# Seven products instead of eight for the queries of the first two units of an attention and low-rank layer

## The chip, the cores and the metric

The kernel runs on one core of a Trainium2 chip. The metric is the device time of one execution in microseconds (us); the median of three runs of the kernel before is 826.52 us (826.05 to 826.85). The engines of the core are TensorE (PE, with its weight loads as PEld), VectorE (DVE), ScalarE (ACT), GpSimd (POOL) and SyncE (SP), which here only issues transfers. Each engine works through its own instructions in the order in which they were written; engines wait for each other on semaphores.

## The reference

Two sequences of 512 tokens with 512 features pass a post-norm layer in float32:

```python
q = hidden_states @ Wq + bq          # 32 heads of 128
k = hidden_states @ Wk + bk          # 8 groups of 128, four heads share one
v = hidden_states @ Wv + bv
q = _rope(q, pos); k = _rope(k, pos)
ctx = softmax(causal(q @ k.T / sqrt(128))) @ v
x = layernorm(x + ctx @ Wo + bo)
y = x @ W_base.T + b_base            # plus low-rank terms of four active experts,
x = layernorm(x + y + contribs * alpha)  # weighted by a softmax of log(prior) + logits
```

## The kernel before, in words

**Units and slots.** A unit u is one group of heads in one of the two batches; there are 16, each with four heads of queries (R = 4). After a setup part, the order of all work is written out by hand: the function `slot(T)` issues, for each time slot T from -8 on, a few matrix products for PE and the small work of the other engines that belongs to them. The table `extra`, filled by `put(slot, f)`, adds work at the end of a slot. A unit's sixteen score blocks lie in slots 16u to 16u + 15; slots get longer as the causal width grows from 32 to 512 columns. Queries are projected about a unit ahead (`T + 24`), Wo's part of a unit begins at slot 16u + 21 (`wo_from`).

**Queries by eight or by seven products.** The queries of two heads are a 2 x 2 block product: weights (two heads by two halves of the features) times x (two halves of the features by two halves of the tokens). From unit 2 on this is done with seven block products instead of eight (`q_products`, steps numbered 1 to 7; each is two matrix products of 256 columns, in four instructions). They need sums of weight blocks (`w_sums`, four POOL instructions; the last overwrites a block of wq) and of x blocks (`x_sums`, four instructions per batch, tile xs). Step 1 begins the PSUM tile qx, step 2 the tile qy; steps 6, 7 and 4 add to qx; step 5 begins qy anew, step 3 adds to it. Between steps, qx is copied to SBUF by ACT (`q_copy`, names p1, u2, u3, c21) and qy is added to a copy by DVE (`q_sum`, names p1, u3, u2). A copy or sum must have read the PSUM tile before the next step overwrites or adds to it:

```python
product(halves[key]["qy"], w[:, 0], xs[:, b, 0], True)      # step 5
nc.vector.tensor_tensor(into, halves[u, k]["qy"], into, ALU.add)   # q_sum
```

The SBUF copies are tiles raw0 (two buffers) and raw1 (one). Units 0 and 1 instead use eight products: `q_mm`, four matrix products of 512 columns per head (two instructions each), in PSUM banks of `q_banks`.

**Rope.** `rope_step` has three parts on DVE (L368, L371, L375), one of which may work in place, and an add on POOL (L376) that writes qT or kT. Queries by eight products are read from PSUM (the program's name is pp), queries by seven from SBUF (name q).

**Setup.** SP issues the loads of x (first batch, four tiles), Wk, Wq of pair 0, the rope tables, Wq of pair 1, Wv, x of the second batch and more, in this order. POOL clears the tiles zt and then issues six small transfers: act_e, four of act_er, act_p, the indices of the active experts. PE transposes x of the first batch and projects K of unit 0; DVE does K's rope; `expert_rows` (eleven DVE instructions of integers, L232 to L252) makes row numbers out of act_e, act_er and act_p, and POOL gathers prior and router bias with them. Then the four heads of unit 0 are projected and roped, with V tiles 0 to 3 (`v_tile` on PE, `v_out` on ACT) and the transposes of the second batch in between. `gather_experts`, six gathers on POOL, is in slot -8.

**Other work around.** `prior_weights` has three steps: a logarithm on ACT, three small DVE instructions, and a small product on PE whose result DVE copies. They stand in slots -4, -3 and -2. `lora_weights` is in slots 12 and 16. V tiles 4 to 7 (second batch) stand in slots -1, 1, 3 and 5; Wv's next load, into the same buffer, in slot 6. `x_sums` of the first batch stand in slots 0 to 3, of the second in 12 to 15, on DVE. In slots 2 to 9 POOL adds bo to the eight tiles of x_sb (L885). `wo_sums` are four sums of Wo blocks per set of weights (L627). Sets 0 to 5 serve two units, the last four sets ("single") one unit each; `wo_sums` of sets 6 and 7 run on POOL one slot before the unit's Wo products, those of sets 0 to 5 on DVE.

Of the kernel before, what the change touches and what calls it, by code (L numbers as in the profile page):

```python
# [9 lines left out]
F32 = mybir.dt.float32  # L10
# [5 lines left out]
P = 128  # L16
# [13 lines left out]
def postln_layer_kernel(  # L30
# [248 lines left out]

    def lora_weights(step):  # L280
        if step == 0:
            ta = ps_wo.tile([P, KC, EAR + EA], F32, tag="wx", name="ta")
            for c in range(KC):
                nc.tensor.transpose(ta[:, c, :], ar_act[:, ts(c, P)], ident[: EAR + EA, : EAR + EA])
            nc.vector.tensor_copy(arT, ta)
            nc.vector.tensor_copy(b_jar, b_act.rearrange("p a (j r) -> p j a r", r=RK))
        else:

            tbm = ps_wo.tile([EAR, BJ, P], F32, tag="wx", name="tbm")
# [6 lines left out]
    def prior_weights(step):  # L296

        if step == 0:
            pr_eps = setup.tile([EA, 1], F32, name="pr_eps")
            nc.vector.tensor_scalar(pr_eps, pr_act, PRIOR_EPS, None, ALU.add)  # L300
            pr["lp"] = setup.tile([EA, 1], F32, name="lp")
            nc.scalar.activation(pr["lp"], pr_eps, AF.Ln)
        elif step == 1:
            lpb = setup.tile([EA, 1], F32, name="lpb")
            nc.vector.tensor_tensor(lpb, pr["lp"], rb_act, ALU.add)
            ones = setup.tile([EA, P], F32, name="ones")
            nc.vector.memset(ones, 1.0)
            pr["rep"] = setup.tile([EA, P], F32, name="lp_rep")
            nc.vector.tensor_scalar(pr["rep"], ones, lpb, None, ALU.mult)
        else:  # L310
            pl = ps_wo.tile([P, EA], F32, tag="wx", name="pl")
# [78 lines left out]
            k_of(u)  # L390
        rope_step(("k", u), H + unit(u)[0], part, kT[u])

    def q_mm(u, r, c, pool, tag):

        g, b = unit(u)
        proj_mm(("q", u, r), pool, tag, wqk["q", set_of(u), r // 2], ts(r % 2, D), b, c)

# [8 lines left out]
    ws = {}  # L406
    halves = {}

    def x_sums(b, step):
        b11, b12, b21, b22 = (  # L410
            xT[:, CH * k : CH * (k + 1), b * S + a * TH : b * S + (a + 1) * TH] for k in range(2) for a in range(2))
        t1, t2, t3, t4 = (xs[:, b, k] for k in range(4))
        nc.vector.tensor_tensor(
            *((t1, b12, b11), (t2, b22, t1), (t3, b22, b12), (t4, b21, t2))[step], ALU.subtract)

    def w_block(n, k, head, c_half):
# [450 lines left out]
        for c in range(KC):  # L867
            v_mm(gg, t, c, pool, tag)

    put(T_BEGIN, gather_experts)  # L870
    for n, gg, t in [(2 * t - 1, 0, TPB + t) for t in range(TPB)] + [(2 * t + 11, 1, t) for t in range(TPB)]:
        put(n, lambda gg=gg, t=t: v_tile(gg, t, ps_wo, "wx"))
        put(n + 1, lambda gg=gg, t=t: v_out(gg, t))
    for n in range(TPB):
        put(n, lambda n=n: x_sums(0, n))
        put(n + 12, lambda n=n: x_sums(1, n))
    for k in range(3):
        put(-4 + k, lambda k=k: prior_weights(k))
        if k < 2:
            put(12 + 4 * k, lambda k=k: lora_weights(k))  # L880
    put(1, lambda: load_q(1, 1))
    put(6, lambda: load_wv(1))
    put(17, lambda: load_wo(1))
    for t in range(NT):
        put(2 + t, lambda t=t: nc.gpsimd.tensor_tensor(x_sb[:, t, :], x_sb[:, t, :], bo_bc, ALU.add))  # L885

    def q_from(u, k):

# [38 lines left out]
    for n in range(NSETS - 2):  # L927
        single = len(set_units(n)) == 1
        for k in range(4):
            put(wo_from(set_units(n)[0]) + (-1 if single else (0, 1, 1, 3)[k]),  # L930
                lambda n=n, k=k, engine=nc.gpsimd if single else nc.vector: wo_sums(n, k, engine))


    weigh_at = {}
# [13 lines left out]
    def slot(T):  # L948

        uq, step = divmod(T + 24, UNIT)  # L950
        kq, step = divmod(step, 8)
        now = B <= uq < NU
        if now and step != 7 and step != 4:
            q_products(uq, kq, {0: 2, 1: 6, 2: 5, 3: 7, 5: 4, 6: 3}[step])
        un, kn = (uq, 1) if kq == 0 else (uq + 1, 0)
        if B <= un < NU and step == 7:
            q_products(un, kn, 1)
        plain_q = T - T_BEGIN < UNIT and divmod(T - T_BEGIN, QB)
        if plain_q:
            r, c = plain_q  # L960
            q_mm(1, r, c, *q_banks[r])
        uk, l = divmod(T + UNIT, UNIT)
        if 0 < uk < PLAIN_K and l < KC:
            k_mm(uk, l)
        kv, o = kv_at(T)
        if kv and o in KV_STEPS:
            kv_products(*kv, KV_STEPS[o])
        kw, sw = divmod(T - LAG_WO, 8)
        products = 0 <= kw < LAST // 8
        if products:  # L970
            wo_products(kw, sw)
# [12 lines left out]
        if kv and KV_OUT.get(o) in KV_ON_ACT:  # L984
            kv_out(*kv, KV_OUT[o])
        for part, j in weigh_at.get(T - 1, ()):
            if j == parts[part][1]:
                context_out(part)

        if 0 <= T - 3 < T_END:  # L990
            normalise(T - 3)
        if 0 <= T - 1 < T_END:
            masked_max(T - 1)
            exponentials(T - 1)
        if products:
            wo_adds(kw, sw)
        if sw == 0 and 0 < kw <= LAST // 8:
            wo_adds(kw - 1, 8)
        if now and step in (1, 5, 7):
            q_sum(uq, kq, {1: "p1", 5: "u3", 7: "u2"}[step])  # L1000
        if kv and o in KV_OUT and KV_OUT[o] not in KV_ON_ACT:
            kv_out(*kv, KV_OUT[o])
        if 0 <= T - 2 < T_END:
            reciprocals(T - 2)
        if 0 <= T - 4 < T_END:
            blocks_transposed(T - 4)
            if (T - 4) % QB == QB - 1:
                blocks_out((T - 4) // QB)
        if T % QB == 1 and 0 <= T // QB - 2 < NP:
            blocks_in(T // QB - 2)  # L1010
        if 0 <= (T - LAG_WO + 1) // 8 < LAST // 8 and (T - LAG_WO + 1) % 8 == 0:
            ctx_sums((T - LAG_WO + 1) // 8)

        ur, sr = divmod(T + 24 - 7, UNIT)
        kr, sr = divmod(sr, 8)
        if B <= ur < NU and sr < 6:
            q_rope(ur, 2 * kr + (sr < 3), sr % 3)
        r, part = divmod(T - T_BEGIN - QB, QB)
        if 0 <= r < R and part < 3:
# [12 lines left out]
    q_banks = ((ps_q, "qx"), (ps_q, "qy"), (ps_q, "qx"), (ps_wo, "wy"))  # L1032

    idle = ps_sc.tile([P, 2 * P], F32, tag="sc", name="idle")
    for _ in range(3):
# [5 lines left out]
    nc.vector.tensor_copy(bqkT, tb)  # L1041
    for c in range(KC):
        k_mm(0, c)
    for part in range(3):
        k_rope(0, part)
    expert_rows()

    for r in range(R):
        for c in range(KC):
            q_mm(0, r, c, *q_banks[r])  # L1050
        for part in range(3):
            q_rope(0, r, part)
        if r == 2:
            for t in range(TPB, NT):
                transpose_token_tile(xT[:, :, ts(t, P)], x_sb[:, t, :], *spare[t % 2 + 2], nc.scalar.copy)
        elif r:
            v_tile(0, r // 2, *spare[r // 2 * 2])
            v_out(0, r // 2)
    for t in range(2, TPB):
        v_tile(0, t, *spare[t % 2 * 2])  # L1060
        v_out(0, t)

    T_SETUP = 20
    for T in range(T_BEGIN, T_SETUP):
# [189 lines left out]
```

## Time and profile before

| what | value |
|---|---|
| median of the runs (lowest to highest) | 826.52 us (826.05 to 826.85) |
| the profiled execution's own time | 826.17 us |
| its span in the profile | 824.2 us |
| PE, DVE, ACT, POOL busy | 814.9, 598.2, 379.0, 327.8 us |
| 8.0 to 34.6 us (setup after the first transposes): PE, DVE, POOL busy | 26.3, 13.3, 10.6 of 26.6 us |
| 34.6 to 45.5 us (slots -8 to -1): PE, DVE, POOL busy | 10.9, 4.5, 8.8 of 10.9 us |
| 45.5 to 68.2 us (slots 0 to 11): PE, DVE, POOL busy | 22.7, 17.3, 15.8 of 22.7 us |
| 68.2 to 101.4 us: PE, DVE, POOL busy | 33.2, 27.0, 10.8 of 33.2 us |

A line of the profile's lists gives a source line, an engine, an operation, the tile written and the tiles read, and a duration. A line of the chain of work gives the start and the duration in us and what ran; the chain is followed back from the last instruction, at each step to what released it. A line of the waits names who waited for whom, the total in us, how often, and the longest. "[1.31 <-POOL wt L627]" at the end of a line is the idle time before it and what ended that. A line of the transfers ends in the time from issue to landing in us.

### The profile page before, as it was taken

What the parts mean: (1) busy time and instruction counts of PE and PEld (TensorE: products, weight loads), DVE (VectorE), ACT (ScalarE), POOL (GpSimd) and SP (SyncE); (2) the same over time, 40 slices, a digit from 0 to 9 for tenths busy, and PEclk for the clock granted to TensorE, in tenths of its full rate; (3) what the DMA queues carried; (4) which work ended last, traced back from release to release, by engine and by line L of the source; (5) the groups of instructions that cost most, each with busy time, mean ns of one, the idle gap of its engine ahead of it and who ended that gap; (6) DMA issues with size and microseconds to landing.
All of it is one profiled execution on the core that took longest, in us unless ns stands there. A gap on an engine that the chain in (4) does not pass through costs nothing.

```text
span 824.2 us, 11178 instructions
## 1 busy us (share of the span) xinstructions
PE 814.9 (99%) x3381; PEld 596.9 (72%) x3381; DVE 598.2 (73%) x1964; ACT 379.0 (46%) x1058; POOL 327.8 (40%) x374
## 2 busy tenths in 40 slices
PE   9999999999999999999999999999999999999997
PEld 5567777777777778777777878777777777655565
DVE  5368877687879886787867786787867678973445
ACT  1236453553545454545535454445535454563254
POOL 6464343511534445322443245353445626410032
PEclk9999999999999999999999999999999999999999
DMA  9015627445465636364554536365544636474211
GB/s 293 34 50 150 203 73 194 126 121 160 117 177 137 183 90 206 89 159 148 149 146 115 179 90 205 91 187 170 137 136 121 195 84 202 138 254 142 77 38 64
DMA packets 84414, 115.99 MB, mean 141 GB/s; under 512 B 6525, under 2 KB 64237, under 8 KB 82306
## 3 DMA queue, kind: packets, MB, share of 16 engines
q1 hardware_dynamic: 83682, 114.98, 48.3%
q8 instruction: 27, 0.44, 0.2%
q0 software_dynamic: 448, 0.14, 0.2%
q14 instruction: 33, 0.27, 0.1%
q10 hardware_dynamic: 224, 0.16, 0.1%
HBM read 71.21 MB, written 44.04 MB: 140 GB/s over the span
## 4 chain that ended last, share of the span: by engine, by line
PE 94%; DVE 2%; POOL 2%; DMA 1%; ACT 0%; issue 0%; SPq 0%; DVEq 0%; POOLq 0%
PE pc L602 16%; PE sc L546 14%; PE qx L434 11%; PE wx L434 11%; PE qy L434 9%; PE wy L434 8%; PE pp L355 5%; PE kx L434 4%; PE vx L512 4%; PE py L767 3%; PE po L674 3%; PE pv L338 3%; PE tp L275 1%; PE py L808 1%; DMA pT<-db 1%; DMA db<-zt 0%
## 5 line engine op out<-in xcount | busy, mean ns | idle before, releaser
L554 DVE CUSTOM_DVE_ANT_0 sc<-sc,maskw 128x288 f32<-128x288 f32 (+15 forms) x256 | 114.2, 446 | 146.3 <-PE sc L546 144.7
L561 ACT ACTIVATE p<-sc,nmax 128x288 f32<-128x288 f32 (+15 forms) x256 | 124.3, 485 | 202.8 <-DVE nmax L554 180.4
L602 PE MATMUL pc<-pT,v 128*128 128x512 f32 x320 | 165.5, 599 | 0.1
L546 PE MATMUL sc<-kT,qT 128*128 128x160 f32 (+15 forms) x512 | 162.0, 398 | 0.2 <-ACT p L561 0.2
L376 POOL TENSOR_TENSOR qT<-q,t 128x512 f32<-128x512 f32 x56 | 76.5, 1366 | 171.4 <-DVE q L375 171.4
L569 ACT ACTIVATE p<-p,den 128x288 f32<-128x288 f32 (+15 forms) x256 | 133.2, 521 | 0.0
L546 PEld LDWEIGHTS sc<-kT,qT 128*128 128x128 f32 x512 | 95.9, 190 | 23.5 <-issue 9.3
L609 ACT ACTIVATE ctxT<-pc,bqkT 128x512 f32<-128x512 f32 x64 | 44.0, 688 | 117.5 <-PE pc L602 117.5
L421 POOL TENSOR_TENSOR cs<-ctxT 128x256 f32<-128x256 f32 x28 | 22.2, 793 | 157.8 <-PE wy L434 93.7
L577 DVE STREAM_TRANSPOSE zt<-p 128x128 f32<-128x128 f32 (+2 forms) x192 | 81.6, 425 | 0.0
L602 PEld LDWEIGHTS pc<-pT,v 128*128 128x128 f32 x320 | 57.0, 190 | 19.2 <-issue 5.7
L470 ACT COPY q<-qx 128x256 f32<-128x256 f32 x112 | 41.4, 369 | 36.5 <-PE qx L434 36.5
L434 PE MATMUL qx<-xs,wq 128*128 128x256 f32 x224 | 58.0, 381 | 0.0
L434 PE MATMUL wx<-wo,ctxT 128*128 128x256 f32 x224 | 57.6, 379 | 0.0
L434 PEld LDWEIGHTS qx<-xs,wq 128*128 128x128 f32 x224 | 41.4, 190 | 22.3 <-issue 18.4
L579 DVE STREAM_TRANSPOSE zt<-p 128x32 f32<-128x32 f32 (+3 forms) x256 | 57.5, 224 | 0.0
L561 ACT ACTIVATION_READ_ACCUMULATOR p<-sc,nmax 128x1 f32 x256 | 49.8, 195 | 0.0
L434 PEld LDWEIGHTS wx<-wo,ctxT 128*128 128x128 f32 x224 | 42.5, 190 | 7.7 <-issue 1.2
L368 DVE SCALAR_TENSOR_TENSOR t<-q,bqkT,rope_sb 64x512 f32<-64x512 f32 x56 | 45.9, 820 | 1.5
L660 DVE TENSOR_TENSOR x_sb<-wx,x_sb 128x256 f32<-128x256 f32 x112 | 47.0, 420 | 0.0
L371 DVE SCALAR_TENSOR_TENSOR t<-q,bqkT,rope_sb 64x512 f32<-64x512 f32 x56 | 43.4, 775 | 1.3
L565 DVE RECIPROCAL den<-den 128x1 f32<-128x1 f32 x256 | 39.3, 153 | 1.5 <-ACT p L561 1.2
(224 smaller groups left out, 1481.9 us busy)
## 6 DMA issues: line engine op xcount, KB each, us to landing
db<-zt SPq DMA_DIRECT2D x64, 256.0 KB, 3.9
pT<-db SPq DMA_DIRECT2D x16, 1024.0 KB, 4.8
db<-zt SPq DMA_DIRECT2D x64, 192.0 KB, 3.3
pT<-db SPq DMA_DIRECT2D x16, 768.0 KB, 4.3
wq<-in_L_attn_Wq_dram SPq DMA_DIRECT2D x20, 512.0 KB, 5.4
wo<-in_L_attn_Wo_dram SPq DMA_DIRECT2D x10, 1024.0 KB, 8.0
db<-zt SPq DMA_DIRECT2D x64, 128.0 KB, 2.4
pT<-db SPq DMA_DIRECT2D x16, 512.0 KB, 4.1
```

The lines of the kernel that those rows point to most:

```text
L368: nc.vector.scalar_tensor_tensor(t2[lo, :], q[hi, :], b_ap[hi, :], rope_sb[hi, 1, :], ALU.add, ALU.mult)
L376: nc.gpsimd.tensor_tensor(dst, t1[:, :].rearrange("p (n s) -> p n s", s=BLK), t2[:, :].rearrange("p (n s) -> p n s", s=BLK), ALU.add)
L434: nc.tensor.matmul(ps, lhsT=wt[:, c, :], rhs=xt[:, c, :], start=start and c == 0, stop=c == CH - 1, skip_group_check=True)
L546: nc.tensor.matmul(sc[s][:, :w], lhsT=qT[u][:, i * QB + n].rearrange("p r s -> p (r s)"), rhs=kT[u][:].rearrange("p n s -> p (n s)")[:, :w ...
L554: nc.vector.tensor_tensor_reduce(sc[s][:, :w], sc[s][:, :w], maskw[:, S - w :], -SCALE, -MASKED, ALU.add, ALU.min, nmax[s])
L561: nc.scalar.activation(ptile[s][:, :w], sc[s][:, :w], AF.Exp, bias=nmax[s], scale=-1.0, accum_out=rden[s])
L569: nc.scalar.activation(ptile[s][:, :w], ptile[s][:, :w], AF.Copy, scale=rden[s])
L577: nc.vector.transpose(z[:, :, last - i : last, n, :].rearrange("p q j s -> p j q s"), ptile[s][:, : i * P])
L579: nc.vector.transpose(z[:, : n + 1, last, n, :], ptile[s][:, i * P : w])
L602: nc.tensor.matmul(psc[p], lhsT=v_sb[g // VG, b][:, j, ts(g % VG, D)], rhs=pT[p][:, :, ts(j, P)], start=(j == 0), stop=(j == i))
L609: nc.scalar.activation(ctxT[p], psc[p], AF.Identity, bias=bqkT[:, col : col + 1])
L660: nc.vector.tensor_tensor(into, pw[k, bank], into, ALU.add)
```

## The change

Units 0 and 1 get their queries by the seven products too; `q_mm` and `q_banks` are gone. In the setup part, the x sums of the first batch (DVE), the weight sums of both pairs (POOL) and `expert_rows` come ahead of the first product; K's rope of unit 0 moves into the second pair; the x sums of the second batch go to POOL, between rope adds. The second batch is transposed after the first pair, and V tile 4 is made in the setup part too (`v_first`). One head's rope of unit 0 goes to slots -8 to -6. In the slots, V tiles 5 to 7 stand in slots -4, 4 and 6, `prior_weights` steps 1 and 2 in slots 9 and 10 (step 0 in the setup part), `gather_experts` in slot -5, the bo adds in slots 12 to 19. Three small PSUM tiles change their bank from wx to wy. Of `wo_sums` of sets 6 and 7, the first two steps go to DVE, the first in the slot before, the other three one slot later than they were.

```diff
-    def q_mm(u, r, c, pool, tag):
-
-        g, b = unit(u)
-        proj_mm(("q", u, r), pool, tag, wqk["q", set_of(u), r // 2], ts(r % 2, D), b, c)
-
...
-    def x_sums(b, step):
+    def x_sums(b, step, engine=nc.vector):
...
-        nc.vector.tensor_tensor(
+        engine.tensor_tensor(
...
-    put(T_BEGIN, gather_experts)
-    for n, gg, t in [(2 * t - 1, 0, TPB + t) for t in range(TPB)] + [(2 * t + 11, 1, t) for t in range(TPB)]:
+    put(T_BEGIN + 3, gather_experts)
+    for n, gg, t in [(n, 0, TPB + 1 + k) for k, n in enumerate((-4, 4, 6))] + [(2 * t + 11, 1, t) for t in range(TPB)]:
...
-    for n in range(TPB):
-        put(n, lambda n=n: x_sums(0, n))
-        put(n + 12, lambda n=n: x_sums(1, n))
-    for k in range(3):
-        put(-4 + k, lambda k=k: prior_weights(k))
-        if k < 2:
-            put(12 + 4 * k, lambda k=k: lora_weights(k))
+    for k in range(2):
+        put(9 + k, lambda k=k: prior_weights(k + 1))
+        put(12 + 4 * k, lambda k=k: lora_weights(k))
...
-        put(2 + t, lambda t=t: nc.gpsimd.tensor_tensor(x_sb[:, t, :], x_sb[:, t, :], bo_bc, ALU.add))
+        put(12 + t, lambda t=t: nc.gpsimd.tensor_tensor(x_sb[:, t, :], x_sb[:, t, :], bo_bc, ALU.add))
...
-            put(wo_from(set_units(n)[0]) + (-1 if single else (0, 1, 1, 3)[k]),
-                lambda n=n, k=k, engine=nc.gpsimd if single else nc.vector: wo_sums(n, k, engine))
+            put(wo_from(set_units(n)[0]) + ((-1, 0, 0, 0) if single else (0, 1, 1, 3))[k],
+                lambda n=n, k=k, engine=nc.gpsimd if single and k > 1 else nc.vector: wo_sums(n, k, engine))
...
-        now = B <= uq < NU
+        now = 0 < uq < NU
...
-        if B <= un < NU and step == 7:
+        if un < NU and step == 7:
             q_products(un, kn, 1)
-        plain_q = T - T_BEGIN < UNIT and divmod(T - T_BEGIN, QB)
-        if plain_q:
-            r, c = plain_q
-            q_mm(1, r, c, *q_banks[r])
...
-        if B <= ur < NU and sr < 6:
+        if 0 < ur < NU and sr < 6:
             q_rope(ur, 2 * kr + (sr < 3), sr % 3)
-        r, part = divmod(T - T_BEGIN - QB, QB)
-        if 0 <= r < R and part < 3:
-            q_rope(1, r, part)
...
-    for part in range(3):
-        k_rope(0, part)
+    for n in range(4):
+        x_sums(0, n)
+    w_sums(0, 0)
     expert_rows()
-
-    for r in range(R):
-        for c in range(KC):
-            q_mm(0, r, c, *q_banks[r])
+    w_sums(0, 1)
+
+
+    def v_first(t):
+        v_tile(0, t, *spare[t % 2])
+        v_out(0, t)
+
+    for k in range(2):
+        for step in (1, 2, 6, 5, 7):
+            q_products(0, k, step)
+            if step == 1:
+                q_copy(0, k, "p1")
+            elif step == 2:
+                q_sum(0, k, "p1")
+                if k:
+                    for part in range(3):
+                        k_rope(0, part)
+            elif step == 6:
+                q_copy(0, k, "u2")
+            elif step == 7:
+                q_copy(0, k, "u3")
+        q_sum(0, k, "u3")
+        if k:
+            x_sums(1, 2, nc.gpsimd)
+            x_sums(1, 3, nc.gpsimd)
+        v_first(2 * k)
+        q_products(0, k, 4)
+        q_copy(0, k, "c21")
+        if k:
+            prior_weights(0)
+            for part in range(2):
+                q_rope(0, 3, part)
+        q_products(0, k, 3)
+        q_sum(0, k, "u2")
+        v_first(2 * k + 1)
+        if k == 0:
+            for t in range(TPB, NT):
+                transpose_token_tile(
+                    xT[:, :, ts(t, P)], x_sb[:, t, :], *spare[(2, 3, 0, 3)[t - TPB]], nc.scalar.copy)
+        for part in range(2 * k, 3):
+            q_rope(0, 2 * k + 1, part)
+        if k == 0:
+            x_sums(1, 0, nc.gpsimd)
         for part in range(3):
-            q_rope(0, r, part)
...
+            if k:
+                put(T_BEGIN + part, lambda part=part: q_rope(0, 2, part))
+            else:
+                q_rope(0, 0, part)
+        if k == 0:
+            x_sums(1, 1, nc.gpsimd)
+    v_first(TPB)
+    q_products(1, 0, 1)
```

More of the change, by code (lines that the diff above doesn't have):

```diff
@@ L281, in lora_weights @@
         if step == 0:
-            ta = ps_wo.tile([P, KC, EAR + EA], F32, tag="wx", name="ta")
+            ta = ps_wo.tile([P, KC, EAR + EA], F32, tag="wy", name="ta")
             for c in range(KC):
@@ L287, in lora_weights @@
         else:
-            tbm = ps_wo.tile([EAR, BJ, P], F32, tag="wx", name="tbm")
+            tbm = ps_wo.tile([EAR, BJ, P], F32, tag="wy", name="tbm")
             for j in range(BJ):
@@ L310, in prior_weights @@
         else:
-            pl = ps_wo.tile([P, EA], F32, tag="wx", name="pl")
+            pl = ps_wo.tile([P, EA], F32, tag="wy", name="pl")
             nc.tensor.matmul(pl, lhsT=pr["rep"], rhs=ident[:EA, :EA], start=True, stop=True)
@@ L1031, in postln_layer_kernel @@
     spare = ((ps_wo, "wx"), (ps_wo, "wy"), (ps_ctx, "ctx"), (ps_sc, "sc"))
-    q_banks = ((ps_q, "qx"), (ps_q, "qy"), (ps_q, "qx"), (ps_wo, "wy"))
     idle = ps_sc.tile([P, 2 * P], F32, tag="sc", name="idle")
@@ L1043, in postln_layer_kernel @@
         k_mm(0, c)
-    for part in range(3):
-        k_rope(0, part)
+    for n in range(4):
+        x_sums(0, n)
+    w_sums(0, 0)
     expert_rows()
-    for r in range(R):
-        for c in range(KC):
-            q_mm(0, r, c, *q_banks[r])
-        for part in range(3):
-            q_rope(0, r, part)
[L1053 to L1061, printed above, removed]
+    w_sums(0, 1)
[38 more added lines that the diff above has]
+            x_sums(1, 0, nc.gpsimd)
+        for part in range(3):
+            if k:
[6 more added lines that the diff above has]
+    q_products(1, 0, 1)
     T_SETUP = 20
```

## The prediction

> **What bounds the kernel now.** I read the page first, then TensorE's waits, then the chain of work in order of time through the first 130 us, then what DVE, POOL and the transfers do there.
>
> ```profile
> span 824.2 us, 11178 instructions
> PE 814.9 (99%) x3381; PEld 596.9 (72%) x3381; DVE 598.2 (73%) x1964; ACT 379.0 (46%) x1058; POOL 327.8 (40%) x374
> PE 94%; DVE 2%; POOL 2%; DMA 1%; ACT 0%; issue 0%; SPq 0%; DVEq 0%; POOLq 0%
> ```
>
> TensorE (PE) is busy for all but 9 us and holds 94% of the chain. So an edit pays by the matmul time that it removes, and costs only where PE then waits. PE's waits, with total, number and longest:
>
> ```profile
> PE wx L434 <- POOL wt L627: 1.3, 1, 1.3
> PE tp L275 <- ACT xT L276: 0.2, 1, 0.2
> ```
>
> The first is late (at 696 us), the second at 24.6 us; the change touches both. From the chain in order of time (start, duration, what):
>
> ```profile
> 60.28 0.86 PE qx L434 x4
> 61.15 0.86 PE pp L355 x2
> ...
> 98.67 1.67 DVE wo L627
> ...
> 101.33 0.04 issue
> 101.38 1.13 PE qy L434 x4
> ```
>
> One 512-column product (two instructions) takes 0.86 us, as does one "product" of the seven (four instructions of 256 columns). And from 92.2 to 101.3 us the chain is DVE's, without a gap: whatever delays DVE there delays PE.
>
> [...] DVE first, POOL second:
>
> ```profile
> 93.45 0.76 DVE L368 SCALAR_TENSOR_TENSOR t<-pp,bqkT,rope_sb 64x512 f32<-64x512 f32 x1
> ...
> 98.59 1.75 DVE L627 TENSOR_TENSOR wo<-wo 128x512 f32<-128x512 f32 x1
> ```
> ```profile
> 93.50 1.27 POOL L376 TENSOR_TENSOR qT<-q,t 128x512 f32<-128x512 f32 x1 [2.08 <-DVE q L375]
> 98.15 1.64 POOL L376 TENSOR_TENSOR kT<-t,t 128x512 f32<-128x512 f32 x1 [3.38 <-DVE t L375]
> ```
>
> A rope step out of PSUM (pp) runs beside a POOL add and still takes 0.76; a difference of two SBUF blocks takes 1.75 instead of some 0.68 while one runs. [...] the trace has 1.27 against 0.69 for 128x512. [...] the trace has 1.28 at 35.0 us, on an idle ACT.
>
> **The products.** Per unit, 16 x 0.86 = 13.76 becomes 14 x 0.86 = 12.04. Two units: -3.44 us. This is sure, since PE is the bound here.
>
> **The first pair's wait.** Nothing holds PE until product 5. K(0) still ends at 11.57, where the first product of wq stands now; products 1, 2 and 6 follow, 3 x 0.86, to 14.15. Product 6 needs s2 from POOL (free at 9.4, two sums of 0.73, some waiting on DVE's x sums: about 11.7) and the x sums (from 8.0, four of 0.7 and a wait: 12.3). But product 5 overwrites qy, which q_sum "p1" must have read; q_sum is on DVE, and in front of it stand now the integer instructions of expert_rows, which K's rope used to shield. They need act_p:
>
> ```profile
> 8.64 0.59 POOL L218 DMA_DIRECT2D act_p<-in_L_ffn_active_dram  x1
> ```
> ```profile
> act_p<-in_L_ffn_active_dram POOLq DMA_DIRECT2D x1, 2.0 KB, 6.3
> ```
> ```profile
> 15.36 0.15 DVE L232 TENSOR_SCALAR lift_p<-act_p 128x4 int32<-128x4 int32 x1
> ...
> 16.12 0.16 DVE L252 CUSTOM_DVE_ANT_0 idx_b<-lane,row_b 128x8 uint16<-128x8 uint16 x1
> 16.30 0.76 DVE L368 SCALAR_TENSOR_TENSOR t<-pp,bqkT,rope_sb 64x512 f32<-64x512 f32 x1
> ```
>
> It lands at 8.64 + 6.3 = 14.9 (the transfers ahead of it don't change). From lift_p to the next instruction 0.94 pass, then q_sum takes 0.4: 16.3. PE waits from 14.1: +2.2 us (2.0 to 2.4). POOL's two gathers and the second w_sums end by 19.5, needed at 26.7: nothing.
>
> **The second pair and the second batch.** PE then: product 5 at 16.3, 7, V(0), 4, 3, V(1), to 23.2; the four transposes to 24.95, with four free banks, so the old 0.24 us wait goes: -0.24. The ACT copies end at 25.9. DVE: u2's sum to 21.9, rope of head 1 to 24.1, rope of head 0 next. These ropes read q from SBUF, no longer PSUM. POOL's add of head 1 (1.27) and x_sums(1, 0) (1.27, ready at 25.9) fall between the three steps of head 0; with one POOL instruction ahead of each of two steps, head 0 ends at 28.8 instead of 26.4. q_sum "p1" of the second pair follows, at 29.2; its product 5 is due at 27.5. Full price 1.7; with one collision 0.45. I take +1.2 (0.4 to 1.8). The other x sums are ready before slot -8. Ln's table load lies under V(3).
>
> **Slots -8 to 12.** Unit 1 now has seven products there, eight slots of 0.86 and V(5) in slot -4; the V moves are work moved under products that have no partner in that slot: nothing, as long as wv(1) lands in the 7.0 us between V(7) and slot 11 (five products of 0.86 and scores of 0.43 to 0.65; the 512 KB issued at 42.1 took 3.9). The four x sums on DVE in slots 0 to 3 go, also four in 12 to 15: no gain, DVE had slack there. Behind the six gathers (33.3 to 40.5 before, 7.2 us) POOL has w_sums (3.2 us) and head 1's add of unit 1. ACT's copy "u3" of pair 1 in slot 4 needs that add (raw1 has one buffer), and product 4 in slot 5 needs the copy. Counted from the start of slot -8: the last rope of unit 0 is added by 4.1, gathers 11.4, w_sums 14.6, add 15.9, copy 16.3. PE comes to product 4 after slots -8 to -1 (7 x 0.86 + 1.73 = 7.75), 0 to 3 (eight of 0.86 for q and K, four scores: 7.6) and 4 (a score and V(6), 2.0): 17.4. That is 1.1 ahead; three collisions of 0.7 make it 1.0 late. In slots 7 to 10 DVE has one rope, the maximum, transposes, two sums and prior's three instructions (0.55) in slots of 1.3 to 1.5 us: it falls some 2 us behind, and prior's matmul (0.35, moved, not added) may wait 0.6. PE waits give DVE time back, so these don't add up: +0.5 (0 to 2.0). If the cover of the slack is gone, all of 2.0 shows.
>
> **The bo adds.** Eight POOL adds of 1.27 go from slots 2-9 to 12-19. Five run in POOL's idle 70 to 86 us. The last three stand behind head 1's add of unit 2 in slot 17 and in front of ctx_sums and head 0's add, which slide 3.8 us into DVE's gapless stretch; ctx_sums is still in time (needed at 99.9, there by about 95). A rope step, one head's rope and a Wo sum there can each wait for a POOL instruction: +0.6 (0 to 1.5).
>
> **Wo sums of the two single sets.** Two of four go from POOL to DVE. At unit 13 the first runs on DVE at 690.3 (behind a POOL sum) to 691.0, then slot 229's maximum, sums, transposes and K rope (2.3 and a collision of 0.6), then the second behind POOL's add of 1.27: 695.2 to 695.9. PE wants it at 696.0, so the 1.31 us wait goes; but DVE carries 1.4 us more and its maxima come later. -0.7 (-1.3 to 0). At unit 12 PE didn't wait: nothing.
>
> Sum: -3.44 + 2.2 - 0.24 + 1.2 + 0.5 + 0.6 - 0.7 = +0.1. On the profiled execution: span 824.2 to 824.3, with the 2.0 us around it 826.3 (826.17 before). The median of the runs is 0.35 above that execution: 826.6.
>
> **Rivals.**
> *Collisions seldom bite.* For: over the whole kernel the rope steps out of SBUF have medians of 750 and 745 ns, as out of PSUM. Against: there POOL's add seldom meets a rope step, here they stand one behind the other. 826.5 - 3.44 + 2.2 - 0.24 + 0.4 - 1.3 = 824.1.
> *The act rows don't hold DVE*, because they land before DVE arrives. For: before, no wait shows at lift_p. Against: DVE got there only at 15.4. Without the 2.2: 824.4, with the first rival too 821.9.
> [...] Unit 0's and 1's ropes now have two SBUF inputs, beside more POOL work. The three terms of 1.2, 0.5 and 0.6 become 1.8 + 2.0 + 1.5 = 5.3, so +3.1: 829.6. It decides once their sum passes 3.8 us instead of 2.3. For: steps of kT's rope at L371 have a mean of 1188 ns. Against: PE's waits give slack back.
>
> **How the numbers follow.** About 0.2%, 1.65 us, is what a measurement of this kernel can tell from no change. My forecast, inside it, 0.42; its own range 824.9 to 828.2. Collisions seldom 0.22, act rows don't hold 0.11: faster 0.33. Full price 0.25: slower. The range leaves out the fastest combination and the end of the slow case: 823.6 to 829.4.
>
> **What would show it.** In the profile after: 28 more four-instruction products of q and no 512-column products of wq; PE waiting about 2 us near 14 to 16 us for DVE's q sum; a second such wait of 0.5 to 1.7 near 28 to 29; rope steps of 1.2 us and more beside POOL; no wait on wt near 696. I am wrong if PE has no wait at 14 us, if slots 4 to 12 or 22 to 24 hold waits beyond 2 us, or if the stretch from 101 us to the end moves by more than 1.5.

## The result, and the profile after

The changed kernel takes 830.88 us (median of 13 runs, 827.42 to 833.01), the kernel before 826.4 us (826.0 to 827.11, 13 runs): 1.0044 times as long, 95% interval 1.0031 to 1.0056. A second series of the changed kernel gave 828.96 us (827.04 to 832.72, 14 runs), ratio 1.0032, interval 1.0016 to 1.0047. So it is slower, by 2.6 us in one series and 4.5 in the other. The predicted 826.6 us was too low; the first median lies above the predicted range, which ended at 829.4, the second inside it.

The runs of the changed kernel spread over 6 us, with 14 of these 27 above 829 us; of the kernel before 5 of 67 in the second series were. The execution that was profiled after is its shortest, 827.42 us. One trace therefore does not explain the median; three further executions of the same kernel were traced (below). None of the nine runs above 831 us has a trace.

The page of the kernel after, the lines that answer to those shown of before: span, busy time of the engines, shares of the chain.

```profile
span 825.6 us, 11322 instructions
PE 813.1 (98%) x3429; PEld 606.0 (73%) x3429; DVE 608.5 (74%) x1976; ACT 384.6 (47%) x1074; POOL 337.4 (41%) x382
PE 90%; DVE 6%; POOL 1%; DMA 1%; issue 1%; ACT 0%; DVEq 0%; POOLq 0%
```

PE has less to do and yet the span is 1.4 us longer: DVE's share of the chain rose from 2% to 6%. PE's waits, with total, number and longest:

```profile
PE qy L430 <- DVE q L470: 3.5, 4, 1.3
PE pl L313 <- DVE lp_rep L310: 0.8, 1, 0.8
PE wx L430 <- DVE den L561: 0.7, 1, 0.7
```

Where the four waits on q's sum stand is seen in PE's own list (start, duration, what, idle time before it and its cause):

```profile
15.63 1.13 PE L430 MATMUL qy<-xs,ws 128*128 128x256 f32 x4 [1.00 <-DVE q L470]
28.39 1.13 PE L430 MATMUL qy<-xs,ws 128*128 128x256 f32 x4 [1.25 <-DVE q L470]
57.30 1.13 PE L430 MATMUL qy<-xT,ws 128*128 128x256 f32 x4 [0.18 <-DVE q L470]
66.83 0.38 PE L313 MATMUL pl<-ident,lp_rep 4*128 4x4 f32 x2 [0.80 <-DVE lp_rep L310]
103.17 1.13 PE L430 MATMUL qy<-xT,wq 128*128 128x256 f32 x4 [1.03 <-DVE q L470]
702.45 1.10 PE L430 MATMUL wx<-wo,ctxT 128*128 128x256 f32 x4 [0.68 <-DVE den L561]
```

All these are places that the prediction named. Each product behind a wait on q takes 1.13 us where one in a row of products takes 0.86, so such a wait costs its own length and 0.27 us. The one at 103.17 us is an exception: the prediction's line at 101.38 us shows that this product took 1.13 before, too, where it began just as DVE's sum ended, so only its wait is new. The chain, in order of time, shows the first of them as foreseen, act_p's transfer first, then the rows, then q's sum:

```profile
8.64 5.53 DMA act_p<-in_L_ffn_active_dram
14.19 0.24 DVE lift_p L233
...
15.14 0.44 DVE q L470
15.63 1.13 PE qy L430 x4
```

The wait at prior's matmul comes from a collision, a DVE instruction that takes longer while a POOL instruction runs beside it. In DVE's and in POOL's list:

```profile
65.53 1.25 DVE L310 TENSOR_SCALAR lp_rep<-ones,lpb 4x128 f32<-4x128 f32 x1
```
```profile
65.44 1.26 POOL L377 TENSOR_TENSOR qT<-q,t 128x512 f32<-128x512 f32 x1 [0.72 <-DVE q L376]
```

lp_rep, four partitions of 128 elements, takes as long as the POOL add beside it; before the change it took 0.35.

### The profile page after: what moved, and what is told of

Same layout as the page of the kernel before. It is cut to its first block, busy times and chain, and to the rows that moved or that the text cites. A ratio compares the mean times of both kernels' runs of the same rounds, so it can differ in the third digit from the quotient of the medians.

```text
span 825.6 us, 11322 instructions
## 1 busy us (share of the span) xinstructions
PE 813.1 (98%) x3429; PEld 606.0 (73%) x3429; DVE 608.5 (74%) x1976; ACT 384.6 (47%) x1074; POOL 337.4 (41%) x382
## 4 chain that ended last, share of the span: by engine, by line
PE 90%; DVE 6%; POOL 1%; DMA 1%; issue 1%; ACT 0%; DVEq 0%; POOLq 0%
PE pc L598 16%; PE sc L542 13%; PE qx L430 12%; PE wx L430 11%; PE qy L430 10%; PE wy L430 8%; PE kx L430 4%; PE vx L508 4%; PE py L763 3%; PE po L670 3%; PE pv L339 2%; PE pp L356 1%; DVE t L372 1%; PE py L804 1%; DMA act_p<-in_L_ffn_active_dram 1%
## 5 line engine op out<-in xcount | busy, mean ns | idle before, releaser
L377 POOL TENSOR_TENSOR qT<-q,t 128x512 f32<-128x512 f32 x64 | 88.0, 1375 | 184.4 <-DVE q L376 179.8
L466 ACT COPY q<-qx 128x256 f32<-128x256 f32 x128 | 47.3, 369 | 58.3 <-PE qx L430 54.4
L430 PE MATMUL qx<-xs,wq 128*128 128x256 f32 x256 | 66.5, 382 | 0.0
L430 PEld LDWEIGHTS qx<-xs,wq 128*128 128x128 f32 x256 | 47.2, 190 | 23.2 <-issue 18.4
L369 DVE SCALAR_TENSOR_TENSOR t<-q,bqkT,rope_sb 64x512 f32<-64x512 f32 x64 | 53.3, 833 | 3.8 <-ACT q L466 2.1
L372 DVE SCALAR_TENSOR_TENSOR t<-q,bqkT,rope_sb 64x512 f32<-64x512 f32 x64 | 50.0, 781 | 1.5
L376 DVE SCALAR_TENSOR_TENSOR q<-q,bqkT,rope_sb 128x512 f32<-128x512 f32 x64 | 47.6, 743 | 0.1
L470 DVE TENSOR_TENSOR q<-qy,q 128x256 f32<-128x256 f32 x96 | 39.8, 415 | 10.4 <-PE qy L430 4.1
```

What stands on the lines that cost most here:

```text
L369: nc.vector.scalar_tensor_tensor(t2[lo, :], q[hi, :], b_ap[hi, :], rope_sb[hi, 1, :], ALU.add, ALU.mult)
L372: nc.vector.scalar_tensor_tensor(t2[hi, :], q[lo, :], b_ap[lo, :], rope_sb[lo, 1, :], ALU.add, ALU.mult)
L376: nc.vector.scalar_tensor_tensor(t1, q, b_ap, rope_sb[:, 0, :], ALU.add, ALU.mult)
L377: nc.gpsimd.tensor_tensor(dst, t1[:, :].rearrange("p (n s) -> p n s", s=BLK), t2[:, :].rearrange("p (n s) -> p n s", s=BLK), ALU.add)
L430: nc.tensor.matmul(ps, lhsT=wt[:, c, :], rhs=xt[:, c, :], start=start and c == 0, stop=c == CH - 1, skip_group_check=True)
```

## The experiments

**Other executions of the changed kernel.** First the changed kernel again, in a series, then two single executions, named look2 and look3.

> The changed kernel once more, to see an execution of the longer kind in a trace. Its runs spread from 827.4 to 833.0 us, the kernel before from 826.0 to 827.1, and the mean granted clock of the longer ones is 0.995 to 0.997, not 0.999. Theory A (clock): after TensorE's new waits near 14 to 16 and 27 to 28 us the granted clock is lowered for some microseconds, in some executions; a mean of 0.995 against 0.999 is about 6.6 us at half clock, 3.3 us of time. The longer execution then shows PEclk under 0.9 in some window before 60 us, and products there take 0.43 us per 256 columns instead of 0.215. Theory B (lengths): the wait for act_p varies with its landing by several us, and the clock is a by-product; the longer execution then shows a first wait of 3 to 6 us.

> The changed kernel once more, to see another long execution in a trace. In the trace of the run named again, the fourth x tile landed late (7.7 us) and the K products took 6.07 us instead of 3.54 (half clock from 8 to 15 us), with no first wait at all. Theory A: a long execution has its slow products after the first wait, from 16 us on. Theory C: it has them in the K products, after a late x tile, and the first wait isn't needed for it.

> As the run named look2, once more. Theory A: slow products after the first wait, from 16 us on. Theory C: slow products in K's projection, after a late x tile.

The series is the second one above. Its traced execution (span 828.0 us) had no first wait at all: a late x tile (waits of 0.81 and 1.23 us before its transposes) put K back by 1.2 us, and the eight instructions of K then took 6.07 us instead of 3.70, with a granted clock of 0.50 from 8 to 12 us and of 0.71 from 12 to 16. So one long execution has its slow products in K, not behind the first wait. look3 (span 827.0) repeats the trace after up to 105 us: waits of 1.00, 1.25, 0.18, 0.79 and 1.03 us; it is longer by waits for the transposed scores, a transfer, of 1.1 and 0.37 us. look2 (span 828.5, a run of 830.29 us) has its slow products behind the first wait. PE's list of look2:

```profile
16.88 2.07 PE L430 MATMUL qy<-xs,ws 128*128 128x256 f32 x4 [2.22 <-DVE q L470]
18.75 1.75 PE L430 MATMUL qx<-xs,wq 128*128 128x256 f32 x4
```

and its table by stretches (busy time of PE, PEld, DVE, ACT, POOL, then granted clock, share and rate of the transfers):

```profile
16.00:20.00 4.00, 3.12 (x7) 2.52 (x8) 0.83 (x2) 0.00 (x0) 2.59 (x4) 0.60 1.09 359
20.00:24.00 4.00, 4.00 (x19) 3.51 (x18) 0.43 (x2) 1.12 (x3) 0.00 (x0) 0.97 0.47 172
```

The wait is 2.22 us long, and over the 4 us from 16 to 20 the granted clock is 0.60 (1.00 in the trace after): two products take 2.07 and 1.55 us in the chain (16.88 to 20.50), where the trace after has 1.13 and 0.86. That is 1.6 us on top of the wait. Why 2.22 and not 1.00? DVE's list, last of the rows, in the kernel after and in look2:

```profile
15.06 0.16 DVE L253 CUSTOM_DVE_ANT_0 idx_b<-lane,row_b 128x8 uint16<-128x8 uint16 x1
```
```profile
15.26 1.24 DVE L253 CUSTOM_DVE_ANT_0 idx_b<-lane,row_b 128x8 uint16<-128x8 uint16 x1
```
```profile
15.72 0.74 POOL L417 TENSOR_TENSOR ws<-wq 128x256 f32<-128x256 f32 x1
```

The last line is POOL's, in look2. act_p landed 0.3 us later (5.82 us after its issue, not 5.53). idx_b started 0.2 us later, and ended with POOL's next weight sum (16.46), where in the trace after it was done before that sum began. Why they met is not shown: idx_b started 0.46 us ahead of that sum and takes 0.16 alone, and the chain lists the 1.13 us that it lost as time without a visible cause. In this execution a transfer that landed 0.3 us later went with 1.2 us more of wait, and with 2.8 us of time in all.

**Take the first wait away.** expert_rows goes behind the first pair's u3 sum. Its two POOL gathers go with it, so POOL's second weight sums start at 12.8 us instead of 15.7.

```diff
-    expert_rows()
...
         q_sum(0, k, "u3")
+        if k == 0:
+            expert_rows()
```

> The changed kernel with the integer instructions of the expert rows behind the first pair's third sum on DVE (near 18 us), where act_p has landed; nothing else moves. My theory: the first wait (1.0 us in the changed kernel's trace) goes, and its execution at full clock is 1.0 us shorter, 826.4 against 827.4. Theory A (clock from the two waits together): the spread shrinks to below 2 us and the median falls to 826 to 828. If the second wait alone lowers the clock, the spread stays and the median is 828 to 830. Theory B (lengths): the spread goes altogether, median 826.4.

826.08 us (22 runs), ratio to before 0.9993, interval 0.9984 to 1.0001; 1 of 22 runs above 829 us, where the unchanged order had 6 of 14 on the same chip in the same series. Span 824.0 us. Product 5 follows product 6 without a gap; the other waits stay:

```profile
PE qy L430 <- DVE q L470: 2.5, 3, 1.2
```

The median falls by 2.9 us against the 828.96 us of that series, though the wait in the trace after is 1.00 us and 0.27. What went with it is most of the long executions. Counted from each kernel's own shortest run of a series, more than 2 us above it are 14 of 27 runs of the changed kernel, 2 of 22 here, and 11 of 67 of the kernel before. The rest of the change then comes to -0.3 us against the kernel before.

**Fill the wait instead, and make it again.** In the first kernel two scratch matrix products of 256 columns (0.86 us), whose result nobody reads, stand ahead of product 5 in both pairs of unit 0 of the changed kernel. In the second, rows_later gets four DVE sums into a scratch tile, read by nobody, ahead of its first q sum.

```diff
+            if step == 5:
+                busy = ps_sc.tile([P, 2 * P], F32, tag="sc", name="busy")
+                for _ in range(2):
+                    nc.tensor.matmul(busy, lhsT=maskw[:, :P], rhs=maskw[:, : 2 * P], start=True, stop=True)
```
```diff
+    spin = work.tile([P, S], F32, tag="p", name="spin", bufs=4)
+    for _ in range(4):
+        nc.vector.tensor_tensor(spin, maskw, maskw, ALU.add)
```

> The changed kernel with two more products of zeros and mask values (256 columns, 0.86 us in all), whose result nobody reads, ahead of product 5 of the first pair: TensorE works while it would wait for the first q sum. Theory A: keeping it busy there keeps the clock, so fewer long executions and a median of 827 to 829; if the wait at 27 us is what counts, no change of the spread. Theory B: no change at all, median 830.9, spread 827.4 to 833.

> The kernel of rows_later (median 826.1, two of 22 executions above 828) with four DVE sums of 128x512 into a scratch tile ahead of the first q sum: TensorE waits at product 5 of the first pair again, until about 15.5 us, now for DVE work instead of act_p. Theory A (the wait lowers the clock): most executions are long again, median 828 to 831. Theory C (late x tiles): the wait costs its 1 to 1.5 us, median 827.1 to 827.6, and no more executions above 829 than with rows_later.

busy: 829.45 us (22 runs, 15 above 829), ratio 1.003, interval 1.0021 to 1.0039. Filling brought nothing, and its trace (span 828.9) does not say why: x was late there (0.65 us), K took 5.98 us, and the first wait was covered. It is inconclusive on the clock, the more so as the clock column reads 1.00 from 8 to 16 us in that trace although K took 5.98 us there and not 3.70. later_spin: 828.08 us, ratio 1.002, interval 1.0011 to 1.003: 2.0 us more than rows_later. 7 of 22 runs are more than 2 us above its shortest, against 2 of 22; with so few runs that is a hint. In its trace (span 827.5) the wait is 0.59 us, but K was slow there too (5.40 us, x late by 1.02 us). With K at 3.70 us the wait would be about 2.3 us (0.59 and 1.70; an estimate), so its length alone can be the 2.0 us. The run does not tell the price of a wait's length from that of the clock.

The K products, which the change leaves alone, say more about the clock. PE's list of later_spin, then of the kernel b_bo_only (below):

```profile
6.85 1.36 PE L276 MATMUL tp<-ident,x_sb 128*128 128x128 f32 x8 [1.02 <-DMA x_sb<-_attn_hidden_states_dram]
8.88 5.40 PE L356 MATMUL pp<-xT,wk 128*128 128x512 f32 x8 [0.49 <-ACT xT L277]
```
```profile
6.26 1.31 PE L275 MATMUL tp<-ident,x_sb 128*128 128x128 f32 x8 [1.15 <-DMA x_sb<-_attn_hidden_states_dram]
8.24 3.70 PE L355 MATMUL pp<-xT,wk 128*128 128x512 f32 x8 [0.49 <-ACT xT L276]
```

The waits are nearly the same, and K is slow in one (clock 0.65 from 8 to 12 us, 0.92 from 12 to 16) and not in the other (1.00 in both). In busy K was slow behind 0.65 us of late x, in the kernel gap (below) it was not behind 0.92 (3.70 us). So in these traces the length of a wait does not decide by itself whether the products behind it run slowly; whether the late tile is what slows K is not shown.

**Move one POOL sum out of the second collision.** On top of rows_later, x_sums(1, 0) goes behind head 0's rope, next to x_sums(1, 1).

```diff
-        if k == 0:
-            x_sums(1, 0, nc.gpsimd)
         for part in range(3):
...
         if k == 0:
+            x_sums(1, 0, nc.gpsimd)
             x_sums(1, 1, nc.gpsimd)
```

> The kernel of rows_later with the first x sum of the second batch on POOL behind the second rope of unit 0, no longer between its three steps. Predicted price of that collision: the wait at product 5 of the second pair goes from 1.25 to 0.3 us, so 0.9 to 1.2 us less than rows_later with the slower first product after a wait: 825.0. A rival: the second rope still meets POOL's add of the first, and the x sums, now later, hold up K's rope and the third sum: no gain, 826.1.

825.36 us (22 runs), ratio 0.9989, interval 0.9979 to 0.9999. The collision in question, in the kernel after, DVE's list and POOL's:

```profile
24.66 1.66 DVE L372 SCALAR_TENSOR_TENSOR t<-q,bqkT,rope_sb 64x512 f32<-64x512 f32 x1
26.36 1.64 DVE L376 SCALAR_TENSOR_TENSOR q<-q,bqkT,rope_sb 128x512 f32<-128x512 f32 x1
```
```profile
24.01 1.77 POOL L377 TENSOR_TENSOR qT<-q,t 128x512 f32<-128x512 f32 x1 [5.29 <-DVE q L376]
25.75 1.71 POOL L409 TENSOR_TENSOR xs<-xT 128x512 f32<-128x512 f32 x1
```

Two rope steps of 0.75 take 1.65 each, one behind each POOL instruction. Without the x sum there the second takes 0.75, and the wait of 1.25 us is 0.36.

**The Wo sums alone**, in the kernel before.

```diff
-            put(wo_from(set_units(n)[0]) + (-1 if single else (0, 1, 1, 3)[k]),
-                lambda n=n, k=k, engine=nc.gpsimd if single else nc.vector: wo_sums(n, k, engine))
+            put(wo_from(set_units(n)[0]) + ((-1, 0, 0, 0) if single else (0, 1, 1, 3))[k],
+                lambda n=n, k=k, engine=nc.gpsimd if single and k > 1 else nc.vector: wo_sums(n, k, engine))
```

> The kernel before with only the edit of the Wo sums of the single sets (two of four to DVE, three of four one slot later). Predicted -0.7 (-1.3 to 0); the changed kernel's trace has a wait of 0.68 us for DVE there instead of 1.31 for POOL, so -0.6: 825.8 against 826.4. A rival: DVE's load gives it back within the next slots, 826.4. The spread stays below 1.2 us under either.

825.88 us (22 runs), ratio 0.9994, interval 0.9985 to 1.0003, which includes no change; span 823.5, 0.7 less. The old wait of 1.31 us goes and DVE's later maxima bring one of 0.68 (the line at 702.45 us above). The two recorded waits differ by 0.63, but less is gained. PE's list of the kernel before:

```profile
700.95 1.03 PE L434 MATMUL wx<-wo,ctxT 128*128 128x256 f32 x4
```

The kernel after is 1.79 us later than before ahead of both waits (694.70 against 692.91 at the product qy there), and 1.50 later at this product (702.45), so only 0.3 us are gained: a product between the two waits, before which the profile lists none, is also delayed, by some 0.35 us. The remaining 0.3 to 0.4 us of wo_only's 0.7 are gained at 725 us, where PE takes up transferred scores, not at the Wo sums.

**The bo adds alone, and back.** First in the kernel before, then out of the changed kernel on top of later_sums.

```diff
-        put(2 + t, lambda t=t: nc.gpsimd.tensor_tensor(x_sb[:, t, :], x_sb[:, t, :], bo_bc, ALU.add))
+        put(12 + t, lambda t=t: nc.gpsimd.tensor_tensor(x_sb[:, t, :], x_sb[:, t, :], bo_bc, ALU.add))
```

> The kernel before with one part of the change: the eight bo adds in slots 12 to 19 instead of 2 to 9. If they delay DVE's gapless stretch by themselves (my sixth term): a wait of 0.4 to 1.1 us at the product of 101.38 us, median 0.5 to 1.3 above the kernel before. Rival: the place of the product does it, which this kernel leaves alone: no wait there, within 0.3 of the kernel before.

> The changed kernel with the act rows behind the first pair's u3 sum, x_sums(1, 0) beside x_sums(1, 1), and the eight bo adds back in slots 2 to 9. If the bo adds that slid into DVE's gapless stretch make the wait of 1.03 us near 101 us (my sixth term, there +0.6): that wait goes to under 0.4 and the first product after it takes 0.86 instead of 1.13, so the span falls by 0.8 to 1.3 from 824.4 and the median from 825.4 to about 824.4. Rival: the wait is the place of that product against DVE's work (K of unit 2 starts 0.7 us later against the slots than before, whatever POOL does): then 0.8 to 1.1 stays and the median is 825.4 within 0.5; then POOL has eight adds more in slots 2 to 9 and the wait of 0.18 near 55 us grows to 1 us or more: 826.

b_bo_only: 827.5 us (21 runs), ratio 1.0014, interval 1.0006 to 1.0021; span 825.5. PE's, POOL's and DVE's list:

```profile
102.65 1.13 PE L434 MATMUL qy<-xT,wq 128*128 128x256 f32 x4 [1.03 <-DVE q L474]
```
```profile
88.16 4.17 POOL L885 TENSOR_TENSOR x_sb<-x_sb,bo_bc 128x512 f32<-128x512 f32 x3
```
```profile
91.47 1.40 DVE L371 SCALAR_TENSOR_TENSOR t<-q,bqkT,rope_sb 64x512 f32<-64x512 f32 x1
...
96.47 1.38 DVE L627 TENSOR_TENSOR wt<-wo 128x512 f32<-128x512 f32 x1
```

This is the same wait as in the changed kernel, made by this edit alone: three adds behind head 1's add; beside them and the work that they push back, a rope step and a Wo sum, 0.75 and 0.69 before, take 1.40 and 1.38. The two delays make 1.34 us. The product starts at 102.65 us instead of 101.38, 1.27 later, of which 0.2 is K's later start in this execution. bo_early confirms it from the other side, in PE's list:

```profile
100.75 1.13 PE L430 MATMUL qy<-xT,wq 128*128 128x256 f32 x4
```

The wait is gone. The product still takes 1.13 us, where 0.86 was expected: it did so before the change, too. And the kernel is not faster than later_sums: 825.67 us (14 runs), ratio 0.9997, interval 0.9986 to 1.0007. The adds in slots 2 to 9 now put back POOL's add of kT, which by the profile released ACT's copy out of qx, and PE waits for the copy. PE's list of bo_early:

```profile
61.22 1.13 PE L430 MATMUL qx<-xs,ws 128*128 128x256 f32 x4 [0.77 <-ACT q L466]
```

This is a wait of the kind that the prediction's term for slots -8 to 12 described, at another copy.

**Prior's steps early**, on top of bo_early.

```diff
-        put(9 + k, lambda k=k: prior_weights(k + 1))
+        put(-3 + k, lambda k=k: prior_weights(k + 1))
```

> As bo_early, and prior's two steps in slots -3 and -2 instead of 9 and 10. The wait of 0.8 us at prior's matmul comes from lp_rep, which took 1.25 us beside POOL's add of head 1 (0.35 before the change). If so the wait near 65 us goes, and nothing like it stands in slots -3 to -1 unless POOL is busy there too: the median is 0.5 to 1.1 below bo_early's, about 823.5, under the kernel before by some 2.8. Rival: POOL's gathers and sums fill slots -8 to 0, and lp_rep meets one of them there: 0.5 to 1.2 us of wait in slot -2, no gain against bo_early.

827.67 us (21 runs), ratio 1.0014, interval 1.0007 to 1.0022. The wait at prior's matmul goes (lp_rep took 0.28 us there), and a longer one comes in its place, some 7 us further on:

```profile
71.87 1.13 PE L430 MATMUL qx<-xs,wq 128*128 128x256 f32 x4 [1.78 <-ACT q L466]
```

PE comes to this product some 1.6 us earlier than in bo_early, counted from the products near 55 us: above all, the wait of 0.86 us and prior's matmul behind it are gone. POOL's add that the copy waits for ends 0.9 later, since a weight sum and that add take longer (1.18 for 0.73, 1.75 for 1.27). Neither theory had that. The trace explains only part of the 2.0 us: it is of a short execution (826.21 us), whose span is 0.7 us above bo_early's, 0.3 of it from K's later start. Ten runs lie at 825.98 to 827.03 us with a mean clock of 0.998 or 0.999, eleven from 827.67 on with 0.996 to 0.998. Whether the wait of 1.78 us goes with a lower clock in the longer ones is not shown, as none of them has a trace.

**All work placed where POOL is idle**, on top of later_sums: the bo adds two by two in slots 12 to 15, prior's steps in slots 10 and 11.

```diff
-        put(9 + k, lambda k=k: prior_weights(k + 1))
+        put(10 + k, lambda k=k: prior_weights(k + 1))
...
-        put(12 + t, lambda t=t: nc.gpsimd.tensor_tensor(x_sb[:, t, :], x_sb[:, t, :], bo_bc, ALU.add))
+        put(12 + t // 2, lambda t=t: nc.gpsimd.tensor_tensor(x_sb[:, t, :], x_sb[:, t, :], bo_bc, ALU.add))
```

> The changed kernel with the act rows behind the first pair's u3 sum and x_sums(1, 0) beside x_sums(1, 1), and with the remaining collisions taken out by place alone: the eight bo adds two by two in slots 12 to 15 (POOL stood idle from 76 to 85 us, so they end by about 82, ahead of DVE's gapless stretch and behind slot 4's copy), and prior's two steps in slots 10 and 11 instead of 9 and 10 (lp_rep then stands behind POOL's add of head 1 and not beside it). If the waits were these collisions: none above 0.4 at the products near 61 and 101 us and at prior's matmul near 65; against later_sums (span 824.4, median 825.4) 1.03 + 0.8 of wait and 0.27 for a slowed product go, so a span near 822.3 and a median of 823.0 to 824.0, some 2.5 to 3 under the kernel before. Rival: DVE's backlog of slots 7 to 10, not POOL, makes lp_rep late, or the first pair's long executions remain: then 824.5 or more.

823.85 us (10 runs, 822.92 to 825.61), ratio to before 0.9971, interval 0.996 to 0.9982. It beats both kernels. POOL's adds end at 81.1 us, before head 0's next add at 84.19:

```profile
70.32 10.81 POOL L877 TENSOR_TENSOR x_sb<-x_sb,bo_bc 128x512 f32<-128x512 f32 x8
84.19 1.27 POOL L377 TENSOR_TENSOR qT<-q,t 128x512 f32<-128x512 f32 x1 [3.05 <-DVE q L376]
```

Of the change's waits 0.36 and 0.18 us on q's sum and the 0.68 at 700 us are left, in a span of 822.6 us that also holds 1.3 us of waiting for transferred scores. Its x tiles made PE wait 1.1 us, but K starts only 0.1 us later than in the kernel before.

## Why the prediction was wrong

The terms of the sum, as predicted and as two traces of the changed kernel have them (the shortest execution, and look2), against the kernel before's span of 824.2 us. Where the product behind a wait for q's sum is slower than before, 0.27 us of it is in the term. The bo adds have their wait alone. The term of the Wo sums is read from PE's starts: the product at 103.17 us comes 1.79 us later than before (101.38), the one at 702.45 us, behind the Wo sums, 1.50 later (700.95).

```text
                                    predicted   after   look2
products                              -3.44     -3.44   -3.44   (by count)
start of K (x tiles' landing)          0        +0.30   +0.34
first pair's wait                     +2.2      +1.27   +2.49
  slow products behind it              -         0      +1.63
old wait of the transposes            -0.24     -0.24   -0.24
second pair                           +1.2      +1.52   +1.52
slots -8 to 12                        +0.5      +1.25   +1.25   (0.18 + 0.27 + 0.80)
bo adds                               +0.6      +1.03   +1.03
Wo sums of the single sets            -0.7      -0.3    -0.3
sum                                   +0.1      +1.4    +4.3
span against before's 824.2                     +1.4    +4.3
```

Without the first pair's wait and the start of K, the terms after add up to -0.2 us; rows_later, which lacks that wait, measures -0.3. So the sum closes twice. The step that failed is the pricing of the waits, the first pair's and those of the collisions, not the places where they were foreseen. In the second series the changed kernel is 2.6 us slower, 2.5 above the predicted sum. The first pair's wait accounts for 0.7 of these (2.9 by its removal, for 2.2); by the trace, slots -8 to 12 for 0.75, the bo adds for 0.4, the second pair for 0.3, the Wo sums for 0.4. In the first series 1.9 us more are lost, in long executions; why there are more of them is open.

**The first pair's wait.** Its mechanism was right: the act rows hold q's sum, and product 5 waits for that. Its price was not. The prediction took one landing time, 14.9 us, from the trace of before, and put the wait at 2.0 to 2.4 us, and nothing behind it. act_p landed at about 14.2 and 14.5 us in the two traces; the wait is 1.00 us, or, where the last of the rows meets POOL's next sum, 2.22, and in the second case two products behind it take 2.07 and 1.55 us (granted clock 0.60 from 16 to 20 us). That look2's 2.22 us agree with the prediction is luck: act_p landed 0.4 us earlier than assumed, and a collision that it did not foresee made up for it. The prediction had counted idle time as the whole price of a wait. How the executions split between these cases, and how many of the long ones are of look2's kind and how many start with a late x tile and a slow K, stays open: four traces of the changed kernel are two with a first wait of 1.00 us, look2, and one with a late x tile. Slow K's (5.40 to 6.07 us) came in the traces of three kernels, again, busy and later_spin. But 2 of 22 runs of rows_later were long, with the same loads of x ahead, so late tiles alone do not explain 14 of 27.

**The second pair** was right in mechanism and nearly in size: 1.25 us of wait and 0.27 behind it, predicted 1.2; two collisions at full length. later_sums took out one of them and 0.9 us of the wait. **The Wo sums** gained less than half of what was predicted: the wait went, and the maxima came later as foreseen, but at a higher price. **The bo adds** were mis-sized: 1.03 for +0.6 (1.26 by the medians of b_bo_only). The prediction named the two victims, a rope step and a Wo sum, and discounted them; both hit in full, and as DVE had no gap there, some 1.07 us of their 1.34 in b_bo_only became PE's. **Slots -8 to 12**: 1.25 for +0.5, inside 0 to 2.0, but in part by another way than described. Product 4 did not wait, product 3 behind it 0.18 us, and prior's matmul, which the prediction named, 0.80, not for a backlog but since lp_rep met head 1's add of POOL (1.25 us, 0.35 before). With the bo adds back in slots 2 to 9, a copy's wait of 0.77 us appears.

Not in the sum at all: the product behind a new wait, 0.27 us three times, 0.8 us together. The prediction's line at 101.38 us showed such a product of 1.13 us.

Of the rivals, "collisions seldom bite" fell: they bit in all three terms. "The act rows don't hold DVE" fell; they held it in the traces after, look2 and look3. The slower rival, with each collision at its full price, came nearest with 829.6 us, between the two medians: the three collision terms are 1.52 + 1.25 + 1.03 = 3.80 us, just the sum from which it was to decide, and 1.5 below its 5.3. That its total fits so well is in part luck, since the first pair's wait and the Wo sums cost more than it assumed.

Of the clock, look2 shows slow products (2.07 and 1.55 us where the trace after has 1.13 and 0.86, at a granted clock of 0.60 from 16 to 20 us) behind a wait of 2.22 us, and K was slow behind waits of 0.65 to 1.23 us in three traces (5.40 to 6.07 us for 3.70), while waits of 1.25 us at 28 us and 1.03 at 103 us left the clock at 1.00. What sets the clock is not shown: the length of a wait alone does not decide it in these traces, and a short one was no safeguard.

## What to carry to other kernels

A wait of TensorE is priced by its length, by the slower product behind it (here 1.13 us for 0.86), and by the risk of further slow products, which came in some executions and not in others: 1.6 us of them behind look2's wait of 2.22 us, 1.7 to 2.4 in K behind waits of 0.65 to 1.23. Where a small late transfer feeds a strict queue, its landing time is a spread and not a number (act_p took 5.50 to 5.82 us in three traces of the changed kernel and 6.3 before), so trace several executions before and after. Where DVE has no gap, a DVE instruction that POOL's work can meet is to be priced at the full collision (1.40 and 1.38 us for 0.75 and 0.69 in b_bo_only), and work that can move belongs in a stretch in which the other engine is idle by the trace, as the eight adds between 70 and 81 us. A part of a change that loses can hide one that pays: seven products for eight take 3.4 us less by their count, and the order around them gave that back until the first wait and the collisions were taken out one by one (from 830.88 and 828.96 us to 823.85).

## What was not expected of the hardware

- With a wait of 2.22 us ahead of it, TensorE had a granted clock of 0.60 from 16 to 20 us (look2); behind waits of 1.00 and 1.25 us it had 1.00 (the trace after). Behind nearly equal waits for x, 1.02 and 1.15 us, K took 5.40 us in one trace and 3.70 in another.
- The clock column read 1.00 from 8 to 16 us where the eight instructions of K took 5.98 us instead of 3.70 (the trace of busy).
- A DVE instruction of 128 x 8 elements took 1.24 us beside a POOL sum and 0.16 without; one of 4 x 128 took 1.25 beside a POOL add and 0.27 to 0.35 without. In both cases the DVE instruction ended within 0.1 us of POOL's (16.50 and 16.46; 66.78 and 66.70), so in these two the end of the POOL work set the price, not the length of the DVE instruction.
- A wait of PE had let POOL keep up: with 0.86 us of it and the matmul behind it gone, PE waited 1.78 us at a product some 7 us further on (prior_early).
